# Moving one layer's transposes and a score turn from TensorE to VectorE and DRAM in a four-layer graph network kernel

## The chip, the cores and the metric

The kernel runs on one core of a Trainium2 chip. Its time is device time in microseconds (us), from start to end of one execution. The core has these engines: TensorE (PE in the profile; its weight loads are PEld), VectorE (DVE), ScalarE (ACT), GpSimd (POOL) and SyncE (SP), which here issues all DMA transfers. Each engine works through its own list of instructions in order, and a wait at the head of a list holds up what stands behind it.

## The reference

There are 64 graphs of 256 nodes with 256 features each, and an integer adjacency matrix per graph. Four layers follow each other; each normalises its input, cuts it at zero and adds its result to the state `x`:

```python
h = maximum(layernorm(x), 0); x = x + multihead_attention(h, adj)     # layer 0: 8 heads of 32
h = maximum(layernorm(x), 0); x = x + elu(softmax(mask(leaky(f1 + f2)), axis=1) @ (h @ W))   # layer 1
h = maximum(layernorm(x), 0); x = x + gated(h, adj)                   # layer 2
h = maximum(layernorm(x), 0); x = x + graph_attention(h, adj)         # layer 3: 4 heads of 64
# gated: three rounds of
m = h @ weight[i]; aggr = A.T @ m
r = sigmoid(i_r + h_r); z = sigmoid(i_z + h_z); n = tanh(i_n + r * h_n)
h = (1 - z) * n + z * h        # i_* = aggr @ w_ih.T + b_ih, h_* = h @ w_hh.T + b_hh
```

In layers 1 and 3 a score is the sum of a term of the row's node and a term of the column's node, so one of the two terms must stand along the free axis, on all partitions.

## The kernel before

Everything is float32. Two graphs form a pair, 32 pairs in all. A tile of one pair has 128 partitions and 4 token tiles of 256 features (1024 columns). A float32 matmul shows as two instructions in the trace, a transpose as one.

**The planner.** `Plan.add` records every step as a task with the engines that could do it, an estimated length, the buffers it reads and writes, and a stage name ("2n" is the norm of layer 2, "2z" its z gates). `Plan.order` (from L161) then writes out one order for the whole program: among the tasks that are ready and find free buffers it takes the one that can begin first by its estimates, and among equals the one with the lowest key, which is the pair times `PERIOD` plus a number from the table `KEYS` for stage and kind of engine. Work of several pairs is thus interleaved, and the buffer counts in `SLOTS` (with the spare ones that only the oldest pair may take) say how many pairs can be under way. `w4` are large buffers of 1024 columns, `w2` half ones of 512, `ps` the eight PSUM banks. `Plan.SWITCH` is the estimated price of changing the array mode of TensorE: L782 runs in row groups, L834 in column groups, L1234 in halves, the rest on the whole array.

**The norm.** `norm_relu` takes mean and variance on VectorE (L530, L532), the inverse root on GpSimd (L543, L544), and scales on ScalarE or VectorE (L557, L563). Then layers 0, 2 and 3 turn the tile to put features on partitions: eight 128x128 transposes on TensorE (L602) into two PSUM banks, and an eviction of each (L355 or L356, or with the relu L614 or L615). In layer 2 the relu comes before the turn, as the token form is needed too.

**Turning through DRAM.** The probabilities of layers 0 and 3, and in layer 2 the state between rounds, are turned without TensorE: VectorE transposes the 32x32 blocks of a tile (L672, L693, L1250), SP writes it to DRAM (L661, L1254), and four more transfers read it back with the blocks in their places (L664, L1257). Its readers then find the columns in runs of 32 elements ("mixed" in the code). The last pair turns its layer 2 state on TensorE (L1140).

**The score term.** `to_all` puts a column of scores on all partitions: a transpose on TensorE of 4, 8 or 16 columns (L859), an eviction (L355, L356), a store of the rows to DRAM (L864) and a load that repeats them on every partition (L872). Layer 1 calls it once a pair, layer 3 once, and twice in the last pair.

**Layer 2.** A round computes the bias part of n (stage 2h), sums messages over the graph (2m, L1036), then the gates r, n and z with L1059: eight instructions of 128x512 each for r and z and four each for the two parts of n, for each half `o` of the features. The n gate gets a sum (L1096), a tanh (L1100) and a subtraction h - n into a new tile `u` (L1105, VectorE or GpSimd); z gets a tanh (L1115) and two VectorE steps (L1120, L1125), which make `u` the new state.

Of the kernel before, what the change touches and what calls it, by code (L numbers as in the profile page):

```python
# [17 lines left out]
P = 128  # L18
EPS = 1e-5
MASKED = -1.0e30  # L20
ALPHA = 0.2
# [18 lines left out]
class Plan:  # L40
# [14 lines left out]
    SPARE, GRAIN = 5, 0.001  # L55
# [4 lines left out]
    PERIOD = 2008  # L60
# [3 lines left out]
        ("io", "SP"): -22628, ("w", "SP"): 6160, ("w", "on"): -16051, ("w", "PE"): 28184, ("0n", "on"): -19306,  # L64
        ("0n", "SP"): 5751, ("0n", "PE"): 4447, ("0", "on"): 13647, ("0", "PE"): -689, ("0s", "PE"): -30872,
        ("0s", "on"): 35014, ("0e", "on"): 15593, ("0e", "SP"): 64094, ("0c", "PE"): 582, ("0c", "on"): 67923,
        ("1n", "on"): 13111, ("1n", "SP"): -3349, ("1", "on"): 14867, ("1r", "PE"): 2956, ("1r", "on"): -22849,
        ("1r", "SP"): -28662, ("1e", "on"): 128, ("1c", "PE"): -14716, ("1c", "on"): -29044, ("2n", "on"): -12901,
        ("2n", "SP"): 36028, ("2n", "PE"): 3358, ("2", "on"): -7047, ("2h", "PE"): 8742, ("2h", "on"): 5862,
        ("2m", "on"): -11894, ("2m", "PE"): -1886, ("2r", "PE"): 8465, ("2r", "on"): -17986, ("2u", "PE"): 9750,  # L70
        ("2u", "on"): 12069, ("2z", "PE"): 10422, ("2z", "on"): -12469, ("2b", "on"): 642, ("2b", "SP"): 7700,
        ("3n", "on"): 25987, ("3n", "SP"): 33785, ("3n", "PE"): 6756, ("3", "on"): 2218, ("3", "PE"): -74722,
        ("3r", "on"): -55996, ("3r", "PE"): -624, ("3r", "SP"): 24892, ("3e", "on"): 40995, ("3e", "SP"): 20273,
        ("3c", "PE"): 10928, ("3c", "on"): 2398, ("3b", "on"): -8939, ("3b", "SP"): 23874, ("out", "SP"): -40141,
        ("2b", "PE"): 56777, ("3e", "PE"): -100101, ("3b", "PE"): 38324,
# [7 lines left out]
    def __init__(self, slots, spare):  # L83
        self.slots, self.spare = slots, spare
        self.pairs = []
        self.stage, self.rank = "", None
# [4 lines left out]
    def add(self, forms, reads=(), writes=(), latency=0.0, claims=(), mode="full"):  # L91
# [11 lines left out]
        t.stage, t.mode = self.stage, mode  # L103
# [31 lines left out]
    def order(self):  # L135
# [11 lines left out]
        for t in every:  # L147
            engine = t.forms[0][0]
            kind = engine if engine in ("PE", "SP") else "on"
            t.key = t.rank[0] * self.PERIOD + t.rank[1] * 1e-4 + self.KEYS.get((t.stage, kind), 0.0)  # L150
# [73 lines left out]
def tile_adj_preln_d4(  # L224
# [41 lines left out]
        "x": (5, [P, T * D], FP, 0),  # L266
        "w4": (24, [P, T * D], FP, 5),
        "part": (10, [P, N2], FR, 1),
        "f3": (2, [P, T, E3], FP, 0),
        "mask": (5, [P, T * N], BF, 0),  # L270
        "ps": (8, [P, 512], FP, 2),
        "w2": (4, [P, N2], FP, 1),
        "st": (4, [P, T, 6], FP, 0),
        "mv": (4, [P, T, 2], FP, 1),
        "rs": (4, [P, 2, T], FP, 2),
        "mx": (16, [P, H0], FP, 3),
        "zs": (12, [P, H0], FP, 3),
        "rz": (12, [P, H0], FP, 2),
        "f12": (2, [P, 2, T], FP, 0),
        "rows": (3, [T * H3, P], FP, 2),  # L280
        "dst": (4, [P, T, H3], FP, 3),
        "turn": (8, [P, T * N], FP, 3),
        "turn2": (4, [P, N2], FP, 2),
        "row1": (4, [N2], FP, 3),
        "row3": (4, [H3 * N2], FP, 0),
# [31 lines left out]
    for tag, (n, shape, dtype, _) in SLOTS.items():  # L317
        if tag not in tiles:
            tiles[tag] = [(dram if tag in ("row1", "row3", "turn", "turn2") else work).tile(shape, dtype, name=f"{tag}_{i}") for i in range(n)]
    plan = Plan({tag: v[0] for tag, v in SLOTS.items()}, {tag: v[3] for tag, v in SLOTS.items()})  # L320
# [4 lines left out]
    def w4():  # L325
        return buf("w4")
# [4 lines left out]
    def bank():  # L331
        return buf("ps")
# [183 lines left out]
    TURNED = ("2m",)  # L516
# [226 lines left out]
    def layer0(xt, p):  # L743
# [10 lines left out]
        qT, kT, v, cT = w4(), w4(), w4(), w4()  # L754
# [16 lines left out]
        for g in range(2):  # L771
# [55 lines left out]
            psc = bank()  # L827

            def context(g=g, psc=psc, pT=pT):
# [13 lines left out]
            add(  # L843
                evict(N2, lambda g=g: tok(cT(), N2)[:, :, g * N : (g + 1) * N], lambda psc=psc: tok(psc(), N)),
                reads=[psc], writes=[(cT, g)],
            )
            ps = bank()
            add((PE, 1.74, lambda ps=ps, g=g: graph_mm(ps, cT, wo_sb, g)), reads=[(cT, g), WO], writes=[ps])
# [6 lines left out]
    def to_all(row, src, columns, n, dsts):  # L855

        ps, rows = bank(), buf("rows")
        add(
            (PE, TURN + 0.12, lambda: nc.tensor.transpose(ps()[0:n, 0:P], columns(), ident)),  # L859
            reads=[src], writes=[ps], claims=[rows],  # L860
        )
        add(evict(P, lambda: rows()[0:n, :], lambda: ps()[0:n, 0:P]), reads=[ps], writes=[rows])
        add(
            (SP, 0.7, lambda: nc.sync.dma_start(row().rearrange("(c p) -> c p", p=P)[0:n], rows()[0:n, :])),  # L864
            reads=[rows], writes=[row], latency=1.8,
        )
        for i, dst in enumerate(dsts):

            def spread(i=i, dst=dst):
                n = dst().shape[1]  # L870
                part = row()[i * n : (i + 1) * n]
                nc.sync.dma_start(dst(), bass.AP(tensor=part.tensor, offset=part.offset, ap=[[0, P], [1, n]]))  # L872

            add((SP, 0.7, spread), reads=[row], writes=[dst], latency=4.2)

    def layer1(xt, p):
# [8 lines left out]
        for g in range(2):  # L885

            def dots(g=g):
                for t in (2 * g, 2 * g + 1):
                    for w in range(2):
                        nc.vector.tensor_tensor_reduce(  # L890
                            tok(e(), N)[:, t, :], tok(h())[:, t, :], wa_bc[:, w, :], 1.0, 0.0, ALU.mult, ALU.add, f12()[:, w, t : t + 1])

            add(
                (V, 4 * FUSED, dots, True), reads=[(h, g), W1], writes=[(e, 2 * g), (e, 2 * g + 1), (f12, g)],
            )
        f1 = buf("w2")
        plan.stage = "1r"
        to_all(buf("row1"), f12, lambda: f12()[:, 0], T, [f1])
        for t in range(T):
            g = t // 2  # L900
            add(
                (A, act(N, 1), lambda t=t, g=g: nc.scalar.activation(
                    tok(e(), N)[:, t, :], f1()[:, g * N : (g + 1) * N], AF.Prelu,
                    bias=f12()[:, 1, t : t + 1], alpha=ALPHA)),
                reads=[f1, f12], writes=[(e, t)],
            )
# [82 lines left out]
    def layer2(xt, p):  # L989
# [58 lines left out]
        for l in range(NL):  # L1048
            r, hn, u = w4(), w4(), w4()
# [15 lines left out]
            for o in range(2):  # L1065
                ps = gate(1.72, ((whhT, hT),), (4 + o) * P, o, [r, hn])
# [13 lines left out]
            for o in range(2):  # L1080
                ps = gate(3.44, both, o * P, o, [r])
                add(
                    (A, act(N2, 1), lambda o=o, ps=ps, r=r: nc.scalar.activation(  # L1083
                        at_o(r, o), ps(), AF.Tanh, bias=brz[:, o : o + 1], scale=0.5)),
                    reads=[ps, BN], writes=[(r, o)],
# [3 lines left out]
                        at_o(hn, o), at_o(r, o), 1.0, at_o(hn, o), ALU.add, ALU.mult), True),  # L1089
                    reads=[(r, o)], writes=[(hn, o)],  # L1090
                )
            plan.stage = "2u"
            for o in range(2):
                ps = gate(1.72, ((giT[:, l], aT),), (4 + o) * P, o, [u])
# [10 lines left out]
                    either(0.0, lambda eng, o=o, u=u, hT=hT, hn=hn: eng.tensor_sub(  # L1105
                        *((by_tile(wide(u, o)), wide(hT, o), by_tile(wide(hn, o))) if hT.mixed
                          else (wide(u, o), wide(hT, o), wide(hn, o))))),
                    reads=[hT if hT.mixed else (hT, o), (hn, o)], writes=[(u, o)],
                )

            plan.stage = "2z"
            for o in range(2):
                ps = gate(3.44, both, (2 + o) * P, o)
                add(
                    (A, act(N2, 1), lambda o=o, ps=ps, r=r: nc.scalar.activation(  # L1115
                        at_o(r, o), ps(), AF.Tanh, bias=brz[:, 2 + o : 3 + o], scale=0.5)),
                    reads=[ps], writes=[(r, o)],
                )
                add(
                    (V, dve(N2), lambda o=o, r=r, u=u: nc.vector.scalar_tensor_tensor(  # L1120
                        at_o(u, o), at_o(r, o), 1.0, at_o(u, o), ALU.add, ALU.mult), True),
                    reads=[(r, o)], writes=[(u, o)],
# [3 lines left out]
                        at_o(u, o), at_o(u, o), 0.5, at_o(hn, o), ALU.mult, ALU.add), True),  # L1126
# [5 lines left out]
            if by_dma("2m", p):  # L1132
                turn_chunks(u, h)
# [24 lines left out]
    def layer3(xt, p):  # L1158
# [29 lines left out]
        dst = buf("dst")  # L1188
        for ts, sds in ((slice(0, 2), sd[:1]), (slice(2, 4), sd[1:])) if hT.fine else ((slice(0, T), sd),):
            of = (dst, ts.start) if hT.fine else dst  # L1190
            add(
                (V, 0.09, lambda ts=ts: nc.vector.tensor_copy(dst()[:, ts], f()[:, ts, D + H3 : E3]), True),
                reads=[(f, t) for t in range(ts.start, ts.stop)], writes=[of],
            )
            n = (ts.stop - ts.start) * H3
            to_all(buf("row3"), of, lambda ts=ts: dst()[:, ts].rearrange("p t h -> p (t h)"), n, sds)
# [97 lines left out]
    for p in range(B // 2):  # L1294
        plan.pair()
        plan.stage, xt = "io", buf("x")
# [56 lines left out]
```

## Time and profile before

| | |
|---|---|
| median of 3 runs | 3545.06 us (3544.0 to 3546.97) |
| the profiled execution | 3550.16 us |
| its span, first to last instruction | 3548.4 us |
| granted TensorE clock, mean | 0.994 |
| DMA: read and written in DRAM | 394 MB and 281 MB, 190 GB/s over the span |
| TensorE's largest group, L1059 | 4608 instructions, 50% of the chain that ended last |

The durations in what follows come from that one profiled execution. A group's row gives line, engine, operation, result and operands by the program's names, shapes and count, then the group's busy time and the mean length of one in ns, then how long the engine stood idle before it and what ended that. Matmuls overlap each other, so a mean length can be more than busy time divided by count.

### The profile page before, as it was taken

The numbers are of one execution on the slowest core, as the hardware profiler recorded it, in microseconds if no ns is written. First come the engines' busy times: TensorE is split into PE (matmuls) and PEld (weight loads), VectorE is DVE, ScalarE is ACT, GpSimd is POOL, SyncE is SP. The second block draws the span as 40 slices with busy tenths as digits, with TensorE's granted clock in tenths as the row PEclk, the third lists the DMA queues.
The fourth block names the chain that finished last, engine by engine and source line by source line (L and its number), as shares of the span: only waits on it lengthen the run. The fifth ranks groups of instructions, "written<-read, shape, count | busy, mean of one in ns | idle before, by whom it ended". The sixth has DMA issues, their size and how long they took to land.

```text
span 3548.4 us, 54621 instructions
## 1 busy us (share of the span) xinstructions
PE 3500.6 (99%) x15345; PEld 1965.5 (55%) x15345; DVE 2879.5 (81%) x8769; ACT 2634.5 (74%) x7011; POOL 452.0 (13%) x505
## 2 busy tenths in 40 slices
PE   8999999999999999999999999999999999999996
PEld 5555555555555555555555555555555555555553
DVE  7887688887888878888887878888889887898655
ACT  7887576887678876787877778777788777778555
POOL 2001111111111110111101110011101011111010
PEclk9999999999999999999999999999999999999998
DMA  7755476665767656576565766657577565676534
GB/s 222 212 168 183 130 231 193 214 208 164 226 187 220 208 173 208 184 226 201 183 210 178 241 187 192 219 174 222 182 214 217 180 212 182 200 226 187 164 94 133
DMA packets 544142, 687.69 MB, mean 194 GB/s; under 512 B 86112, under 2 KB 463072, under 8 KB 543840
## 3 DMA queue, kind: packets, MB, share of 16 engines
q1 hardware_dynamic: 543840, 684.21, 63.2%
q8 instruction: 123, 2.02, 0.2%
q14 instruction: 179, 1.47, 0.2%
HBM read 394.28 MB, written 281.35 MB: 190 GB/s over the span
## 4 chain that ended last, share of the span: by engine, by line
PE 89%; DVE 4%; ACT 3%; DMA 2%; SPq 1%; issue 1%; POOL 0%; DVEq 0%; ACTq 0%; POOLq 0%
PE ps L1059 50%; PE ps L761 6%; PE ps L637 6%; PE ps L1036 5%; PE ps L782 4%; PE ps L1234 3%; PE ps L1179 3%; PE ps L834 3%; PE ps L966 3%; PE ps L952 3%; PE ps L602 2%; ACT w L737 1%; DVE w L730 1%; DVE w L672 1%; DMA x<-in_x_dram 1%
## 5 line engine op out<-in xcount | busy, mean ns | idle before, releaser
L1059 PE MATMUL ps<-w,whhT 128*128 128x512 f32 x2304 | 1078.6, 595 | 1.5 <-DVE w L1125 1.5
L1059 PE MATMUL ps<-w,giT 128*128 128x512 f32 x2304 | 1067.3, 592 | 0.0
L737 ACT ACTIVATE w<-w,mx 128x256 f32<-128x256 f32 x1536 | 758.9, 500 | 12.0 <-DVE mx L730 11.6
L1059 PEld LDWEIGHTS ps<-w,giT 128*128 128x128 f32 x2304 | 433.7, 190 | 530.6 <-issue 508.6
L1059 PEld LDWEIGHTS ps<-w,whhT 128*128 128x128 f32 x2304 | 424.0, 190 | 465.9 <-issue 426.3
L355 ACT COPY w<-ps 128x512 f32<-128x512 f32 x574 | 324.4, 581 | 275.1 <-PE ps L761 102.3
L672 DVE STREAM_TRANSPOSE w<-w 128x1024 f32<-128x1024 f32 x380 | 468.7, 1235 | 49.8 <-ACT w L814 30.4
L730 DVE CUSTOM_DVE_ANT_0 w<-ps,mask 128x256 f32<-128x256 f32 x1024 | 369.9, 416 | 54.2 <-PE ps L782 52.7
L814 ACT ACTIVATE w<-w,rz 128x256 f32<-128x256 f32 x672 | 292.8, 503 | 5.8 <-DVE rz L807 5.5
L737 ACT ACTIVATION_READ_ACCUMULATOR w<-w,mx 128x1 f32 x1536 | 295.9, 193 | 0.0
L543 POOL TENSOR_SCALAR rs<-mv 128x4 f32<-128x4 f32 x129 | 41.8, 324 | 1994.5 <-DVE mv L532 1919.4
L557 ACT ACTIVATE w<-x,rs 128x256 f32<-128x256 f32 x466 | 245.0, 591 | 50.3 <-DVE rs L549 50.1
L1115 ACT ACTIVATE w<-ps,brz 128x512 f32<-128x512 f32 x192 | 130.3, 679 | 148.1 <-PE ps L1059 148.1
L1211 ACT ACTIVATE w<-w,f 128x256 f32<-128x256 f32 x512 | 218.7, 498 | 15.8 <-DMA w<-row 15.8
L1036 PE MATMUL ps<-part,part 128*128 128x256 f32 x1536 | 226.0, 299 | 2.1 <-ACT part L1020 1.5
L730 DVE CUSTOM_DVE_ANT_0 w<-w,mask 128x256 f32<-128x256 f32 x512 | 201.9, 438 | 23.3 <-ACT w L1211 23.3
L1105 POOL TENSOR_TENSOR w<-w,w 128x512 f32<-128x512 f32 x84 | 112.8, 1344 | 809.2 <-ACT w L1100 634.6
L1036 PEld LDWEIGHTS ps<-part,part 128*128 128x128 f32 x1536 | 196.1, 191 | 35.6 <-issue 20.1
L1083 ACT ACTIVATE w<-ps,brz 128x512 f32<-128x512 f32 x192 | 130.1, 678 | 112.0 <-PE ps L1059 111.8
L1088 DVE SCALAR_TENSOR_TENSOR w<-w,w 128x512 f32<-128x512 f32 x192 | 136.4, 711 | 87.2 <-ACT w L1069 45.5
L1120 DVE SCALAR_TENSOR_TENSOR w<-w,w 128x512 f32<-128x512 f32 x192 | 141.5, 737 | 80.0 <-ACT w L1115 68.1
L1100 ACT ACTIVATE w<-w,bih_sb 128x512 f32<-128x512 f32 x192 | 135.3, 718 | 85.1 <-DVE w L1096 85.1
(116 smaller groups left out, 5122.1 us busy)
## 6 DMA issues: line engine op xcount, KB each, us to landing
turn<-w SPq DMA_DIRECT2D x473, 512.0 KB, 3.1
w<-turn SPq DMA_DIRECT2D x1892, 128.0 KB, 3.7
w<-in_adj_dram SPq DMA_DIRECT2D x128, 512.0 KB, 5.7
w<-row SPq DMA_DIRECT2D x64, 512.0 KB, 4.9
x<-in_x_dram SPq DMA_DIRECT2D x64, 256.0 KB, 4.3
out_dram<-x SPq DMA_DIRECT2D x64, 256.0 KB, 2.1
turn<-w SPq DMA_DIRECT2D x62, 256.0 KB, 2.0
w<-turn SPq DMA_DIRECT2D x248, 64.0 KB, 2.5
```

Of the source, the lines that this page charges most:

```text
L355: (A, act(n), lambda: nc.scalar.copy(dst(), src())),
L557: nc.scalar.activation(tok(xn())[:, t, :], tok(xt())[:, t, :], func, bias=rs()[:, 1, t : t + 1], scale=rs()[:, 0, t : t + 1])
L637: mm(ps()[:, c * D : (c + 1) * D], chunk(src, k, 2 * g + c), rhs[:, k, :], start=k == 0, stop=k == 1)
L672: add((V, dve(T * N), lambda: nc.vector.transpose(blocks(), blocks())), writes=[e])
L730: nc.vector.tensor_tensor_reduce(row, src, mask, scale, 3.0e38, ALU.add, ALU.min, mn)
L737: nc.scalar.activation(row(e, r), row(e, r), AF.Exp, bias=mn()[:, r : r + 1], scale=-1.0, accum_out=zs()[:, z0(r) : z0(r) + 1])
L761: mm(ps(), w[:, k, o * P : (o + 1) * P], wide(hT, k), start=k == 0, stop=k == 1)
L782: mm(banks[hh]()[:, cc * N : (cc + 1) * N], tok(qT(), N2)[r, cc, t * P : (t + 1) * P], tok(kT(), N2)[r, cc, g * N : (g + 1) * N].rearrange ...
L814: op(row, row, rz()[:, r : r + 1])
L1036: mm(ps()[:, o * N : (o + 1) * N], chunk_of(part(), h.mixed, c, o), tok(ams[g](), N)[:, c, :], start=i == 0 and c == 0, stop=i == 1 and c ...
L1059: mm(ps(), w[:, k, c0 : c0 + P], wide(src, k), start=n == 0, stop=n == 2 * len(terms) - 1)
L1211: nc.scalar.activation(dst, src, AF.Prelu, bias=f()[:, t, D + h : D + h + 1], alpha=ALPHA)
```

## The change

For all pairs but the last, the norm of layer 2 turns its tile with the function `turn_rows`, which was there but not used: a block transpose on VectorE and a trip through DRAM; the two evictions fall away. The gates of round 0 then read the turned tile in runs of 32, and `u` is a tile of its own in that round only; in the others the new state is written over the old one. `to_all` no longer uses TensorE: VectorE transposes the blocks of a 128x32 tile and the store to DRAM picks 32-element runs out of it. The results of the r and z gates go to half buffers, the z gates are listed ahead of the second part of the n gate, and the context of layer 0 goes to a half buffer per graph. Buffer counts, spares, `PERIOD` and all keys are new, and the first pair and the last two have keys of their own.

```diff
-    SPARE, GRAIN = 5, 0.001
+    SPARE, GRAIN = 2, 0.001
...
-    PERIOD = 2008
+    PERIOD = 2538
...
-        ("2u", "on"): 12069, ("2z", "PE"): 10422, ("2z", "on"): -12469, ("2b", "on"): 642, ("2b", "SP"): 7700,
...
+        ("2r<", "on"): -6234, ("2z<", "PE"): 8380, ("2z<", "on"): -1814, ("2u<", "PE"): 8044, ("2u<", "on"): -10808,
...
-            t.key = t.rank[0] * self.PERIOD + t.rank[1] * 1e-4 + self.KEYS.get((t.stage, kind), 0.0)
+            t.key = t.rank[0] * self.PERIOD + t.rank[1] * 1e-4 + self.KEYS.get((t.stage, kind), self.KEYS.get((t.stage.strip("<>"), kind), 0.0))
...
-        "x": (5, [P, T * D], FP, 0),
-        "w4": (24, [P, T * D], FP, 5),
+        "x": (6, [P, T * D], FP, 0),
+        "w4": (22, [P, T * D], FP, 2),
...
-        "mask": (5, [P, T * N], BF, 0),
+        "mask": (6, [P, T * N], BF, 1),
...
-        "w2": (4, [P, N2], FP, 1),
+        "w2": (5, [P, N2], FP, 0),
...
-        "f12": (2, [P, 2, T], FP, 0),
-        "rows": (3, [T * H3, P], FP, 2),
-        "dst": (4, [P, T, H3], FP, 3),
+        "f12": (2, [P, 32], FP, 0),
+        "rows": (3, [P, 32], FP, 2),
+        "dst": (4, [P, 32], FP, 3),
...
-    TURNED = ("2m",)
+    TURNED = ("2", "2m")
...
-        qT, kT, v, cT = w4(), w4(), w4(), w4()
+        qT, kT, v = w4(), w4(), w4()
...
-            psc = bank()
+            psc, cT = bank(), buf("w2")
...
-        ps, rows = bank(), buf("rows")
+        rows = buf("rows")
+        add((V, 0.11, lambda: nc.vector.transpose(rows(), src())), reads=[src], writes=[rows])
         add(
-            (PE, TURN + 0.12, lambda: nc.tensor.transpose(ps()[0:n, 0:P], columns(), ident)),
-            reads=[src], writes=[ps], claims=[rows],
-        )
-        add(evict(P, lambda: rows()[0:n, :], lambda: ps()[0:n, 0:P]), reads=[ps], writes=[rows])
-        add(
-            (SP, 0.7, lambda: nc.sync.dma_start(row().rearrange("(c p) -> c p", p=P)[0:n], rows()[0:n, :])),
-            reads=[rows], writes=[row], latency=1.8,
+            (SP, 0.7, lambda: nc.sync.dma_start(row().rearrange("(j a i) -> a j i", a=4, i=32), rows())),
+            reads=[rows], writes=[row], latency=2.2,
         )
...
-            r, hn, u = w4(), w4(), w4()
+            hn = w4()
...
+                r = buf("w2")
...
+            plan.stage = "2z"
+            zt = [buf("w2") for o in range(2)]
+            for o in range(2):
+                ps = gate(3.44, both, (2 + o) * P, o, [zt[o]])
...
             plan.stage = "2u"
+            u = w4() if hT.mixed else hT
...
-                    reads=[hT if hT.mixed else (hT, o), (hn, o)], writes=[(u, o)],
-                )
...
+                    reads=[(hn, o), *([hT] if hT.mixed else [])], writes=[(u, o)],
+                )
+                add(
+                    (V, dve(N2), lambda o=o, z=zt[o], u=u: nc.vector.scalar_tensor_tensor(
+                        wide(u, o), z(), 1.0, wide(u, o), ALU.add, ALU.mult), True),
+                    reads=[zt[o]], writes=[(u, o)],
+                )
...
+        plan.place = "<" if p == 0 else ">" if p >= B // 2 - 2 else ""
```

The function that the norm of layer 2 now calls:

```python
    def turn_rows(xn):

        e, eT = w4(), w4()
        add(
            (V, dve(T * D), lambda: nc.vector.transpose(
                e().rearrange("p (b x i) -> p x b i", b=4, i=32), xn().rearrange("p (x b j) -> p x b j", b=4, j=32))),
            reads=[xn], writes=[e],
        )
        through_dram(e, eT)
        eT.mixed = True
        return eT
```

## The prediction

> **What bounds the kernel now.** I read the busy shares first, then the busy times by stretch of the span, then TensorE's groups, its timeline, and last the waits.
>
> ```profile
> PE 3500.6 (99%) x15345; PEld 1965.5 (55%) x15345; DVE 2879.5 (81%) x8769; ACT 2634.5 (74%) x7011; POOL 452.0 (13%) x505
> ```
>
> TensorE is busy for 99% of the span, VectorE for 81%. Whether TensorE is bound everywhere is told by the stretches (columns: stretch, its length, then busy time and instructions of each engine, granted clock, DMA share, GB/s):
>
> ```profile
> 0.00:50.00 50.00, 38.06 (x187) 25.84 (x188) 32.79 (x136) 33.85 (x92) 19.65 (x26) 0.93 0.73 232
> 300.00:3300.00 3000.00, 2997.38 (x13074) 1673.85 (x13072) 2483.09 (x7525) 2249.28 (x5985) 391.64 (x431) 1.00 0.65 199
> 3450.00:3548.40 98.40, 71.15 (x292) 39.58 (x290) 57.88 (x176) 57.67 (x156) 9.38 (x12) 0.85 0.48 145
> ```
>
> From 300 to 3300 us TensorE stands still for 2.6 us in 3000, at clock 1.00; VectorE has 17% free, ScalarE 25%, the DMA engines 35%. There time is bought only by giving TensorE less to do. The last 98.4 us hold 27.2 us of idle TensorE, the first 50 hold 11.9: at the ends a chain of single steps decides. The order repeats every 430.6 us for four pairs (the long runs of L1059 start at 1522.50, 1953.13, 2383.77 in the chain), 107.65 us a pair; 32 such are 3444.8, so 103.6 us of the span are ends, weights among them.
>
> **TensorE work that goes.** Two kinds of transpose:
>
> ```profile
> L602 PE MATMUL ps<-ident,w 128*128 128x128 f32 x768 | 104.0, 278 | 12.8 <-ACT w L557 12.7
> ...
> L859 PE MATMUL ps<-ident,f 128*4 128x128 f32 x32 | 8.7, 272 | 0.0
> L859 PE MATMUL ps<-ident,dst 128*16 128x128 f32 x31 | 8.5, 273 | 0.0
> ```
>
> L602 is the norm's transpose in layers 0, 2 and 3: 32 pairs x 3 x 8 = 768. Layer 2's go through VectorE for all pairs but the last: 31 x 8 = 248. A mean of 278 ns is not what one costs, as matmuls overlap; what counts is from start to next start (columns: start, length, engine, line, operation):
>
> ```profile
> 1450.54 1.04 PE L602 MATMUL ps<-ident,w 128*128 128x128 f32 x8
> 1451.41 1.88 PE L1059 MATMUL ps<-w,giT 128*128 128x512 f32 x4
> ```
>
> ```profile
> 3468.58 0.27 PE L859 MATMUL ps<-ident,dst 128*16 128x128 f32 x1
> 3468.69 1.88 PE L1059 MATMUL ps<-w,whhT 128*128 128x512 f32 x4
> ```
>
> Eight take 0.87 us, 0.109 each; one of L859 takes 0.11. The Trainium skill speaks otherwise: "TensorE: Matmul & The Clock Gate", Part 4 (PE-mode transpose), gives about 275 ns for one in a kernel's context. The row has that as a duration, but not as spacing. By 275 ns the 248 + 65 transposes would be 86 us; by the timeline 31 x 0.87 = 27.0 us and 65 x 0.11 = 7.2 us, together **34.2 us**. I take the timeline, since in the saturated stretch the next start is what moves.
>
> **What VectorE, ScalarE and DMA get.** The turned tile costs a block transpose, a write of 512 KB to DRAM and four reads, as the tiles at L672 do now:
>
> ```profile
> L672 DVE STREAM_TRANSPOSE w<-w 128x1024 f32<-128x1024 f32 x380 | 468.7, 1235 | 49.8 <-ACT w L814 30.4
> ```
>
> 31 x 1.235 = 38.3 us on VectorE. The score columns get a 128x32 block transpose; no row has one, so it lies between the 128x16 copy (L1192, 174 ns) and the 128x512 block transpose (L1250, 701 ns); I take 0.2 us as the nearer: 13 us. Gone are 11 copies of rows there (3 us). VectorE comes to about 2879 + 38 + 13 - 3 = 2927 us, 84% of 3505. ScalarE loses 54 copies of rows (13 us) and most of the 62 evictions of 0.58 us: a turned tile of layer 2 had its relu before, and needs none after. Both stay under TensorE, so this costs nothing while their order leaves TensorE fed; were VectorE the bound, it would be +48 us.
>
> A rule speaks against the change: "VectorE: DVE Perf Modes", Rules for kernel authors, sends a 128x128 transpose to TensorE where PSUM will do as its destination. Counting engine time it is right here too: 38.3 us on VectorE for 27.0 on TensorE, a loss of 11. But a free 17% pays for a full 100%, so the sum takes -27.
>
> DMA: 31 x 1 MB = 32.5 MB on 688, near 5%; at 63% busy that makes 66%. SP issues 31 x 5 more, at 0.34 us (write) and 0.43 us (read) each 64 us in all; the block transposes' waits on SP are of the kind it has (L661 behind L672: 582.5 us in 231 waits), and queued behind them are other pairs' loads, whose tiles lie ready early. The rows' stores become 128 pieces of 128 B instead of 4 or 16 of 512 B; landing took 3.0 us and I take 3 to 4, off the path except at the end, where it is +1 against the 1.5 us that the transpose and copy took there (3510.10 to 3511.63).
>
> **A slower operand?** In round 0 of 31 pairs the gates read the turned tile in runs of 32 elements: 31 x 24 = 744 instructions of 0.429 us (L1059: four in 1.72), 319 us. Nearest is L1234, which reads turned probabilities in such runs, two matmuls of 256 columns at a time: 32 took 3.61 us. The dense L637 of 256 columns takes 1.73 for eight, 0.216 each, so 32 dense ones two at a time would take 3.46. The 0.15 between them I put down to the change of array mode, since the dense-reading L782 shows such a loss too. So I take zero. If all of that 4% were the runs', it is +14 us; a gain is excluded, since L1059's dense reads are as fast per column as any row has them.
>
> **State in place, smaller buffers, order.** Rounds 1 and 2 (and 0 of the last pair) now write h - n over h, so that subtraction waits until all z gates have read h; before, it could run ahead. Behind it wait two VectorE operations of its own (L1120 and L1125, 0.74 and 0.70), and on an in-order engine whatever is queued next. The z gates' tanh (0.68) runs beside it, so one round gets 0.1 to 0.7 us longer. Hidden where other pairs feed TensorE; in the last pair I count +2. Gates of r and z move from 24 large buffers to 5 half ones, shared with the context tile: more takers, but short ones; I take zero, and the order rival holds the rest. Changes of array mode: an excursion (L782, L834, L1234) costs about 0.3 us beyond its matmuls (16 of L782, four at a time: 1.07 where 16 x 0.216/4 is 0.86, and 0.09 to enter), and the timeline from 1496 to 1873 has about 6.5 of at most 8 a pair. The new keys may merge or split some: one per pair is 32 x 0.3 = 10 us either way; zero taken.
>
> **The ends.** What TensorE waited for there:
>
> ```profile
> PE ps L602 <- ACT w L557: 12.7, 2, 8.8
> PE ps L682 <- ACT w L737: 12.1, 6, 8.3
> PE ps L1140 <- DVE w L1125: 5.9, 2, 3.8
> ```
>
> The 8.8 is the first load and stays. On the chain of the last 60 us I can name what another order would remove: the z tanh waiting behind exponentials (3492.5 to 3494.4, 1.9), the row load behind a turned tile's store on SP (3514.6 to 3515.8, 1.2), GpSimd for an add that VectorE does in half (0.6), the row path (1.5, less 1 for the pieces); in the first 130 us, waits of 2.1, 1.2 and 0.7. That is 8.2, say 8. Bounds: a lengthening of 4, the in-place chain's 2 and as much again from the order, and at best 20, about half of the 39 us idle in both stretches. I take -8 + 2 = **-6**.
>
> **Sum.** On the profiled execution (3550.16 us, span 3548.4): -27.0 - 7.2 - 6 = -40.2, to 3510. It lay 5.1 us above the median of the runs; from 3545.06 the same sum gives **3505 us**.
>
> **Rivals.** (1) As summed, ends between +4 and -18: 3493 to 3515, 0.58. (2) The strided reads do cost: 3505 + 14 = 3519, 0.16; for it, that no full-array matmul reads so yet; against it, L1234. (3) The order gains more: two excursions a pair merged, or the ends halved, 3505 - 19 = 3486, 0.19; for it, 103.6 us at the ends; against it, that two score groups together need all eight PSUM banks. (4) Slower: the turned tile comes late. The path is 1.24 + 3.1 + 3.7 us and queueing, against some 2 us, so about 8 us later; with nothing else to do TensorE would lose 31 x 8 = 248 us, and 3545 - 40 + 248 = 3753. It decides from 40.2/31 = 1.3 us of lost time a pair. Against it stand the turned tiles there are:
>
> ```profile
>   PEld ps L1234: 3.5, 6
>   PEld ps L834: 3.4, 5
> ```
>
> In 535 such tiles TensorE's loads waited 6.9 us, 0.013 each, so 31 more are 0.4 us. For it: SP is in order, and buffers of the large kind are fewer. 0.07: slower 0.04, the same 0.02, still faster 0.01.
>
> **Numbers.** A run can tell about 0.2% (7 us) from no change. Cases 1 to 3 are all faster: 0.93 + 0.01. The range 3482 to 3522 leaves out the high end of (2) and the low end of (3), 0.05 each, and (4): 0.17.
>
> **What would show it.** L602 falls to 520, L859 is gone, TensorE's matmul count falls by 313; the repeat falls from 430.6 to 4 x (107.65 - 0.87 - 0.22) = 426.2 per four pairs, less or more by excursions; four strided L1059 still start 1.72 us apart; VectorE near 84%; idle TensorE still under 5 us between 300 and 3250. Waits of TensorE on the turned tile, a repeat above 430, or a last stretch longer than now would prove me wrong.

## The result and the profile after

The changed kernel takes 3518.77 us in the median (3518.36 to 3519.41, 4 runs), the kernel before 3545.71 us beside it (4 runs): a ratio of 0.9924, 95% interval 0.9907 to 0.9942. That is 27 us less; 40 were forecast. The profiled execution took 3519.16 us with a span of 3517.4. The busy times of the engines after:

```profile
PE 3457.1 (98%) x15032; PEld 1944.5 (55%) x15032; DVE 2873.1 (82%) x8732; ACT 2674.8 (76%) x7097; POOL 347.9 (10%) x435
```

TensorE has 313 instructions less, as many as were to go, but its idle time has not shrunk: 3517.4 - 3457.1 is 60.3 us, against 47.8 before. The stretches of the span after, with the columns as before:

```profile
0.00:50.00 50.00, 41.39 (x190) 27.73 (x191) 34.67 (x134) 31.83 (x81) 21.16 (x28) 1.00 0.75 242
50.00:300.00 250.00, 229.98 (x1145) 134.73 (x1144) 203.99 (x658) 185.29 (x524) 12.91 (x16) 0.97 0.61 186
300.00:3300.00 3000.00, 2998.21 (x13031) 1681.12 (x13030) 2503.53 (x7586) 2338.83 (x6200) 297.31 (x372) 1.00 0.67 211
3450.00:3517.40 67.40, 39.04 (x157) 21.36 (x155) 36.91 (x124) 41.65 (x119) 5.91 (x7) 0.76 0.41 131
```

The second row has to be seen beside the same stretch of the kernel before:

```profile
50.00:300.00 250.00, 245.79 (x1292) 147.13 (x1291) 215.36 (x701) 210.48 (x594) 22.39 (x27) 0.99 0.68 200
```

From 300 to 3300 us TensorE is as full as it was. Between 50 and 300 us it now idles 20.0 us for 4.2, and its granted clock is 0.97 for 0.99. What became of the transposes, in TensorE's and VectorE's groups after (L627 is L602 before; L731 and L889 are the new block transposes):

```profile
L627 PE MATMUL ps<-ident,w 128*128 128x128 f32 x520 | 70.9, 279 | 14.1 <-ACT w L582 14.0
...
L731 DVE STREAM_TRANSPOSE w<-w 128x1024 f32<-128x1024 f32 x31 | 38.3, 1236 | 0.8 <-ACT w L582 0.8
...
L889 DVE STREAM_TRANSPOSE rows<-dst 128x32 f32<-128x32 f32 x33 | 6.8, 206 | 0.3
L889 DVE STREAM_TRANSPOSE rows<-f 128x32 f32<-128x32 f32 x32 | 6.5, 202 | 0.0
```

768 transposes have become 520, the score transposes (L859 before) are gone, and the small block transpose takes 0.2 us. The repeat, read from the chain of work that ended last (start, length, what):

```profile
1009.73 24.04 PE ps L1087 x56
1048.74 20.60 PE ps L1087 x48
1115.75 24.04 PE ps L1087 x56
```

The order now repeats with every pair, each 106.02 us, for 107.65 before: 1.63 us less where 1.09 was to go. And 56 instructions of L1087 still take 24.04 us, 0.429 each. The strided reads of round 0 are no slower: from 500 to 3000 us no L1087 that follows another starts more than 0.434 us after it.

**An account of TensorE's time.** To see where the time went I count, in stretches of 50 us, each matmul at its spacing in a full stretch (512 columns 0.429 us, 256 columns 0.216, 264 columns 0.223, the graph sums of L1036 or L1064 0.126, row and column groups 0.054, halves 0.108, transposes 0.109, and so on), and call that useful; the rest of the stretch is lost, be it idle, a changed mode or a lower clock. (Those graph sums run in the type fp32r, so not everything in the kernel is plain float32.) An excursion is a run of matmuls in row groups, column groups or halves; the first gate is the start of L1059 or L1087 for the first pair.

| us | useful | lost to 300 us | lost 300 to 3300 | lost after 3300 | mode excursions, 500 to 3000 us | first layer 2 gate |
|---|---|---|---|---|---|---|
| before | 3398.2 | 35.6 | 69.9 | 44.6 | 151 | 141.0 |
| after | 3364.0 | 54.4 | 54.9 | 44.1 | 117 | 172.9 |
| difference | -34.2 | +18.8 | -15.0 | -0.5 | | |

The sum is -30.9, and the spans differ by 31.0. The useful work falls by just the 34.2 us forecast because the count prices the transposes at the same 0.109 us: it shows that the work is gone, and e5 below tests the price. The lost time fell by 15.0 in the middle and rose by 18.8 at the start.

### The profile page after: what moved, and what is told of

Its sections match the earlier page's. It is cut to its first block, busy times and chain, and to the rows that moved or that the text cites. A ratio compares the mean times of both kernels' runs of the same rounds, so it can differ in the third digit from the quotient of the medians.

```text
span 3517.4 us, 54023 instructions
## 1 busy us (share of the span) xinstructions
PE 3457.1 (98%) x15032; PEld 1944.5 (55%) x15032; DVE 2873.1 (82%) x8732; ACT 2674.8 (76%) x7097; POOL 347.9 (10%) x435
## 4 chain that ended last, share of the span: by engine, by line
PE 90%; DVE 2%; ACT 1%; DMA 1%; issue 0%; SPq 0%; POOL 0%; DVEq 0%; ACTq 0%
PE ps L1087 54%; PE ps L1064 5%; PE ps L786 5%; PE ps L807 3%; PE ps L1209 3%; PE ps L1263 3%; PE ps L980 3%; PE ps L859 3%; PE ps L994 3%; PE ps L662 3%; PE ps L874 3%; PE ps L627 1%; DMA w<-turn 1%; DVE w L755 0%; ACT w L762 0%; DVE w L697 0%
## 5 line engine op out<-in xcount | busy, mean ns | idle before, releaser
L1087 PE MATMUL ps<-w,whhT 128*128 128x512 f32 x2304 | 1067.7, 593 | 1.5 <-DMA w<-turn 1.5
L1087 PE MATMUL ps<-w,giT 128*128 128x512 f32 x2304 | 1058.3, 592 | 0.7 <-ACT w L380 0.7
L1087 PEld LDWEIGHTS ps<-w,giT 128*128 128x128 f32 x2304 | 436.8, 190 | 544.6 <-issue 527.9
L1087 PEld LDWEIGHTS ps<-w,whhT 128*128 128x128 f32 x2304 | 426.2, 190 | 467.5 <-issue 430.9
L380 ACT COPY w<-ps 128x512 f32<-128x512 f32 (+1 forms) x519 | 295.1, 580 | 290.7 <-PE ps L786 119.3
L839 ACT ACTIVATE w<-w,rz 128x256 f32<-128x256 f32 x782 | 341.9, 508 | 4.5 <-DVE rz L832 4.4
L1135 DVE TENSOR_TENSOR w<-ps,w 128x512 f32<-128x512 f32 x192 | 129.4, 674 | 209.1 <-PE ps L1087 208.5
L568 POOL TENSOR_SCALAR rs<-mv 128x4 f32<-128x4 f32 x129 | 32.5, 252 | 2703.1 <-DVE mv L557 2680.1
L582 ACT ACTIVATE w<-x,rs 128x256 f32<-128x256 f32 x492 | 257.4, 605 | 16.3 <-DVE rs L574 16.1
L1064 PE MATMUL ps<-part,part 128*128 128x256 f32 x1536 | 236.5, 303 | 5.3 <-DVE part L1022 4.3
L1064 PEld LDWEIGHTS ps<-part,part 128*128 128x128 f32 x1536 | 199.5, 190 | 41.2 <-issue 28.2
L755 DVE CUSTOM_DVE_ANT_0 w<-w,mask 128x256 f32<-128x256 f32 x512 | 195.4, 427 | 18.8 <-ACT w L1240 16.6
L555 DVE BATCH_NORM_STATS2 st<-x 128x6 f32<-128x256 f32 x512 | 188.8, 410 | 2.8 <-DMA x<-in_x_dram 2.3
L1117 DVE SCALAR_TENSOR_TENSOR w<-w,w 128x512 f32<-128x512 f32 x192 | 130.3, 679 | 60.5 <-ACT w L1112 58.0
```

The costliest lines, as they stand in the source:

```text
L380: (A, act(n), lambda: nc.scalar.copy(dst(), src())),
L555: nc.vector.bn_stats(st()[:, t, :], tok(xt())[:, t, :])
L582: nc.scalar.activation(tok(xn())[:, t, :], tok(xt())[:, t, :], func, bias=rs()[:, 1, t : t + 1], scale=rs()[:, 0, t : t + 1])
L755: nc.vector.tensor_tensor_reduce(row, src, mask, scale, 3.0e38, ALU.add, ALU.min, mn)
L839: op(row, row, rz()[:, r : r + 1])
L1064: mm(ps()[:, o * N : (o + 1) * N], chunk_of(part(), h.mixed, c, o), tok(ams[g](), N)[:, c, :], start=i == 0 and c == 0, stop=i == 1 and c ...
```

## The experiments

The theories: (A) useful work and lost time add up, and the new loss at the start comes from the new order; (B) the turned tile's trip through DRAM makes it, or takes back what TensorE saves; (C) the first pair's own keys make it; (D) the keys are fitted to one program, and a disturbed order loses TensorE time, whatever is moved. (D) was formed after the first four runs. The figures of lost time in the expectations come from an earlier count that took matmuls on a stretch's border twice; it had 117 where the table's sum is 150 for the kernel before, and the differences are much the same. Every run below has the kernel before beside it on its chip, at 3546 to 3547 us.

| run | median us | ratio, 95% interval | lost to 300 | 300 to 3300 | after 3300 | first gate |
|---|---|---|---|---|---|---|
| e1 parts only | 3656.21 | 1.0306 (1.0288 to 1.0323) | 51.4 | 173.1 | 69.2 | 152.9 |
| e2 unturned | 3607.67 | 1.0172 (1.0157 to 1.0188) | 45.0 | 121.1 | 48.9 | 156.2 |
| e3 first pair as middle | 3607.29 | 1.0170 (1.0154 to 1.0185) | 54.0 | 138.3 | 50.7 | 172.6 |
| e4 last pairs as middle | 3525.45 | 0.9941 (0.9926 to 0.9956) | 53.3 | 53.9 | 53.3 | 171.9 |
| e5 dummy turns | 3542.80 | 0.9989 (0.9982 to 0.9995) | 50.2 | 53.2 | 43.0 | 172.0 |
| e6 other period | 3624.22 | 1.0214 (1.0199 to 1.0229) | 33.9 | 134.3 | 54.9 | 139.6 |
| e7 mode switch | 3540.40 | 0.9986 (0.9977 to 0.9994) | 53.3 | 67.8 | 44.4 | 171.1 |
| e8 control of e7 | 3533.03 | 0.9960 (0.9946 to 0.9975) | 55.4 | 60.0 | 42.9 | 175.0 |
| e9 parts, keys anew | 3544.80 | 0.9993 (0.9983 to 1.0003) | 50.2 | 80.1 | 48.1 | 146.0 |
| e10 first on TensorE | 3527.69 | 0.9946 (0.9931 to 0.9961) | 46.4 | 65.9 | 45.1 | 156.1 |
| e11 VectorE twice | 3542.32 | 0.9990 (0.9980 to 0.9999) | 58.4 | 75.7 | 44.6 | 175.2 |

**e1: the two moves alone.** The kernel before with `to_all` on VectorE as changed, and

```diff
-    TURNED = ("2m",)
+    TURNED = ("2", "2m")
```

> The kernel before with only the two transposes moved (layer 2's tile, score columns), its own keys, buffers and gate order. Theory A (useful TensorE work and lost time add up; the loss at the start comes from the new order, not from the moved work): 34 us less useful work, lost time stays near 117 us, first layer 2 gate near 141 to 150 us, 3511 us. Theory B (the turned tile's trip through DRAM delays layer 2 at the start): lost time before 300 us rises from 33 to about 52, first gate near 165 to 175, 3530 us.

Measured 3656 us: slower than before by 110, and both theories are wrong. The useful work is 3363.4, as low as after the change, so the saving is there; but the middle loses 103 us more than in the kernel before; 60 of it is idle TensorE (2937.2 us busy for 2997.4), and its granted clock there was 0.99 for 1.00. Of what TensorE waited for in its first 300 us, the second row is new:

```profile
PE ps L605 <- ACT w L560: 8.6, 1, 8.6
PE ps L1058 <- DMA w<-turn: 7.4, 1, 7.4
```

The first gate of layer 2 waits once, 7.4 us, for the turned tile. From 300 to 3300 us the longest waits are of other kinds. None of the gates waits on the tile, but the context of layer 3 (L1232) waits on turned probabilities, and no matmul of it did before:

```profile
PE ps L1058 <- DVE w L1124: 12.3, 6, 4.4
PE ps L605 <- ACT w L560: 9.4, 7, 7.4
PE ps L1035 <- DVE part L993: 9.0, 7, 3.2
PE ps L1232 <- DMA w<-turn: 6.0, 3, 4.4
```

**e2: the changed kernel with the tile back on TensorE** (`TURNED = ("2m",)`).

> The changed kernel with layer 2's tile turned on TensorE again (248 transposes come back), all else as changed. Theory A: 27 us more useful work, the start as in the changed kernel (first gate near 173, about 52 us lost before 300), 3546 us. Theory B: the start recovers (first gate near 145, 33 us lost), so 27 - 19 = +8, 3527 us.

Measured 3608 us, 62 more than (A) has. The start recovers by 9.4 us, half of the 18.8, so there (B) is half right. The middle loses 66 us more, though layer 2's tile no longer goes to DRAM: this loss cannot be its trip's.

**e3: no own keys for the first pair** (the weights keep theirs).

```diff
-        plan.place = "<" if p == 0 else ">" if p >= B // 2 - 2 else ""
+        plan.place = ">" if p >= B // 2 - 2 else ""
```

> The changed kernel without the first pair's own keys (it takes those of the middle pairs; weights keep theirs). Theory C (those keys hold layer 2 of the first pair back): first gate before 160 us, lost before 300 us near 35, about 3500 us. Theory A with the cause in depth and middle keys: the start stays as bad or gets worse, 3519 to 3535 us. Steady period 106.0 us in both.

Measured 3607 us with the same work in every instruction, and the period was not kept. The start is unchanged (54.0, first gate 172.6), so (C) falls. The keys of one pair cost 88 us, nearly all of it hundreds of us later. TensorE's busy time in the middle of e3:

```profile
1000.00:2000.00 1000.00, 982.01 (x4226) 548.72 (x4225) 824.44 (x2488) 760.44 (x2024) 138.27 (x151) 1.00 0.68 208
```

and of the changed kernel in the same stretch:

```profile
1000.00:2000.00 1000.00, 1000.00 (x4373) 563.49 (x4372) 834.68 (x2562) 794.57 (x2120) 93.27 (x119) 1.00 0.68 215
```

In e3 147 instructions fewer get done in the 1000 us. By the code of `Plan.order` each choice depends on what came free before, so another start can lead to another sequence for good; that this is the path is argued, and the trace shows the later loss alone.

**e4: no own keys for the last two pairs** (`plan.place` only for the first).

> The changed kernel without the own keys of the last two pairs. If they earn their keep: lost time after 3300 us rises from 41 to over 50, about 3530 us. If they do nothing: within 5 us of 3519. The start and the period of 106.0 us stay.

Measured 3525 us, 6.7 more than with these keys. The two intervals overlap, but the count puts the difference at the end: it loses 53.3 us without them and 44.1 with them, as the kernel before does.

**e5: eight transposes put back at a fixed order.** In the order of the changed kernel, ahead of a gate of round 0:

```diff
+                    if extra:
+                        for j in range(8):
+                            nc.tensor.transpose(ps()[:, (j % 4) * P : (j % 4 + 1) * P], h0()[:, j * P : (j + 1) * P], ident)
```

> The changed kernel in its own order, with eight extra 128x128 transposes on TensorE in 31 pairs, into a bank that the matmuls after them overwrite; the planner does not know of them. Theory A (in a full stretch the spacing of 0.109 us is the price): 31 x 0.87 = +27 us, 3546 us, period 106.0 + 0.87. If a duration of 275 ns each were the price: +68 us, 3587. If TensorE were not the bound: under +5 us.

Measured 3542.8 us, +24 of the 27 expected. The chain gives the period:

```profile
1013.48 24.04 PE ps L1090 x56
1120.36 24.04 PE ps L1090 x56
```

It is 106.88 us, 0.86 more, for eight transposes at 0.109. So in the full stretch the spacing is the price, and not the length of 275 ns.

**e6: the kernel before with another `PERIOD`** (2100 for 2008, no work changed).

> The kernel before with the planner's PERIOD at 2100 for 2008: no work is changed, only the order. Theory D (the keys are fitted to one program, and any disturbance of the order loses TensorE time in the middle, whatever the work): useful work stays at 3432 us, lost time rises from 117 by 40 or more, 3590 us or above. Theory B' (the loss seen when the parts are put in alone comes from the turned tile's wait on DRAM): within 10 us of 3546.

Measured 3624 us: 78 us for one number of the planner, useful work 3398.7, 64 us more lost in the middle. What (D) expected comes, without any moved work. Not every change of keys does it, though: e4 left the middle as it was.

**e7 and e8: the price of an excursion.** One extra small matmul ahead of four gates a pair, in e7 on a column group, in e8 on the whole array:

```diff
+                        mm(ps()[0:32, 0:32], h0()[:, 0:32], h0()[:, 0:32], start=True, stop=True)
```

> The changed kernel in its own order, with four extra excursions to column groups a pair (one 32x32 matmul ahead of four gates, overwritten after), unknown to the planner: 128 in all. At 0.3 us each: +38 us, 3557 us. If excursions cost nothing beyond their matmuls: +5 us or less, as its control.

> The control: the same 128 extra small matmuls on the whole array, no change of mode. +0.06 us each or less: 3519 to 3527 us.

Measured 3540.4 and 3533.0 us, periods 106.77 and 106.46 for 106.02. Both expectations miss: a small matmul on the whole array already costs 0.44/4 = 0.11 us, one on a column group 0.19, so the mode adds 0.08 over its control. A lone small matmul is not a pack of 32, though. What such a pack costs is read from the timeline of the kernel before:

```profile
1473.44 1.04 PE L602 MATMUL ps<-ident,w 128*128 128x128 f32 x8
1474.41 1.93 PE L834 MATMUL ps<-w,w 128*32 128x256 f32 x32
1476.27 3.83 PE L1179 MATMUL ps<-w3a,w 128*128 128x264 f32 x16
1479.93 1.89 PE L637 MATMUL ps<-wo_sb,w 128*128 128x256 f32 x8
```

and of the changed kernel, where both graphs' contexts run as one:

```profile
1300.26 3.60 PE L1087 MATMUL ps<-w,giT 128*128 128x512 f32 x8
1303.79 3.66 PE L859 MATMUL ps<-w,w 128*32 128x256 f32 x64
1307.38 1.99 PE L662 MATMUL ps<-wv_sb,w 128*128 128x256 f32 x8
```

Before, the 32 begin 0.10 us after the eight transposes' 0.87 us are over, they take 1.86 us for 32 x 0.054 = 1.73, and the 16 of L1179 behind them take 3.66 for 16 x 0.223 = 3.57: together 0.3 us beyond the work. The 64 have the same 0.10 to enter and take 3.59 for 3.46. In the median from 500 to 3000 us, entry and leaving included, an excursion costs 0.33 us with 32 matmuls (35 cases before) and with 64 (23 cases after). So the price is one per excursion, a merge saves 0.33 us, and the prediction's 0.3 was right in size. (It was read from L782's row groups, which cost 0.40 in the same count, as what follows them runs 0.10 late; the prediction left that out.) Excursions fell from 6.5 a pair (151 in 2500 us) to 5.0 (117): 1.5 x 0.33 = 0.5 us, which with 0.87 + 0.22 for the transposes makes 1.59 of the 1.63 us of the period.

**e9: the moves alone, with keys searched anew.** The kernel of e1, with the buffers and gate order of the kernel before; no pair has keys of its own.

> The kernel of e1 (the kernel before with only the two transposes moved, its buffers and gate order) with keys searched anew for it, and no own keys for any pair. Theory D (the loss of e1 was the unfitted order): lost time falls from 258 to 110 to 140 us, useful work stays 3399, so 3509 to 3540 us. Theory B (the trip through DRAM takes back what TensorE saves): still above 3546.

Measured 3544.8 us: no different from the kernel before (interval 0.9983 to 1.0003). The new keys took away 111 us of e1's time, so the unfitted order was most of what e1 lost. But useful work is 34.2 us lower than before and lost time 28.3 higher: 14.6 at the start, 10.2 in the middle, 3.5 at the end. The first gate waits for the tile again:

```profile
PE ps L1104 <- DMA w<-turn: 8.1, 1, 8.1
```

**e10: the first pair's tile on TensorE.** The changed kernel with

```diff
-        return l in TURNED and p < B // 2 - 1
+        return l in TURNED and p < B // 2 - 1 and (l != "2" or p >= 1)
```

and keys searched anew.

> The changed kernel with the first pair's layer 2 tile turned on TensorE (0.9 us more useful work) and keys searched anew from its own. Theory B for the start only (the first turned tile comes late when no other pair can feed TensorE): first gate before 165 us, lost before 300 us falls from 52 to 40 to 47, 3508 to 3514 us. Otherwise within 3 us of 3519.

Measured 3527.7 us. At the start it fits (B): 8.0 us less lost, first gate at 156. But the middle lost 11.0 more, and the whole took 8.9 us more than the change in the median (5.1 in the profiled spans; the intervals overlap), where up to 11 less was expected: a miss. Its keys are others throughout, so the 8.0 us are not the tile's alone.

**e11: the block transpose done twice at a fixed order** (31 x 1.23 us more on VectorE).

> The changed kernel in its own order, with the block transpose of layer 2's tile done twice: 31 x 1.23 = 38 us more on VectorE. If free VectorE time pays for it, as the prediction has it: period 106.0, under +6 us in all, most of it at the start. If VectorE's order were on the path: +20 to +38 us.

Measured 3542.3 us, +23.6: the prediction's view fails here. The period is 106.84, 0.82 more, two thirds of what was added. The timeline of TensorE in e11 shows where:

```profile
1184.19 1.88 PE L1088 MATMUL ps<-w,whhT 128*128 128x512 f32 x4
1185.90 0.42 PE L627 MATMUL ps<-ident,w 128*128 128x128 f32 x2
1186.49 0.33 PE L627 MATMUL ps<-ident,w 128*128 128x128 f32 x1 [0.17 <-ACT w L582]
1186.98 0.77 PE L627 MATMUL ps<-ident,w 128*128 128x128 f32 x5 [0.16 <-ACT w L582]
1187.58 1.88 PE L1088 MATMUL ps<-w,whhT 128*128 128x512 f32 x4
```

and the same place in the changed kernel:

```profile
1279.50 1.88 PE L1087 MATMUL ps<-w,whhT 128*128 128x512 f32 x4
1281.21 1.04 PE L627 MATMUL ps<-ident,w 128*128 128x128 f32 x8
1282.09 1.88 PE L1087 MATMUL ps<-w,whhT 128*128 128x512 f32 x4
```

The eight transposes of a norm take 1.68 us for 0.88, as they wait for ScalarE's scaling (L582), which waits for the statistics on VectorE. Everything ahead of them in the period stands at the same distance to 0.01 us. In the changed kernel VectorE runs from 1261.8 to 1281.7 us without a gap ahead of this place, and the new block transpose (1272.66) is in that run. So added VectorE time there moves the norm's statistics, the scaling and then TensorE.

## Why the prediction was right or wrong, point by point

**The total is near the forecast in part by luck.** Between the profiled executions it is -30.9 us for -40.2. The 9.3 us between them are 24.3 missed at the ends less 15.0 in the middle that were taken at zero; that the two misses offset each other was not foreseen.

**The bound and the saved work were right.** TensorE is full from 300 to 3300 us, 313 transposes are gone, and e5 puts 0.86 us a pair back for the 0.87. The Trainium skill's 275 ns ("TensorE: Matmul & The Clock Gate", Part 4) is what one takes from start to end here too (279 in L627's row), and not what a full TensorE saves.

**The strided reads cost nothing**, as taken (0.434 us at most between neighbours). The measured 3519 lies on the number of that rival, but not by its cause.

**"The ends: -6" failed.** They became +18.3, all at the start. I listed waits that another order could remove and did not ask how the new path of the first pair's tile would sit there, though my own rival (4) said that it comes about 8 us later where TensorE has nothing else. In e1 and e9 the first gate waits 7.4 and 8.1 us for it. In the changed kernel about half of the 18.8 us goes when that tile is turned on TensorE (9.4 by e2, 8.0 by e10), but TensorE's waits in the first 300 us show less of it at the gate itself (second row) than at the context of layer 0, which waits for turned probabilities:

```profile
PE ps L859 <- DMA w<-turn: 6.0, 4, 3.8
PE ps L1087 <- DMA w<-turn: 1.5, 1, 1.5
```

In e2 the first row is 2.1 us, and in the kernel before no matmul waits so. All these tiles go through SP's one list; that layer 2's trip holds up the others there is likely, and was not shown. The other half is in the new order's start or in the score turn, which e2 keeps (45.0 for 35.6), and not in the first pair's keys, by e3. The split is not firm: e1 and e9 lose 15.8 and 14.6 us more at the start with the old buffers and gate order. Which of score turn, buffers, spares and middle keys makes the rest was not tried and stays open. At the end the own keys of the last two pairs are worth 6.7 us in the median (9.2 by the count), and that only held the loss where it was.

**"Changes of array mode: zero taken" was mis-sized.** The price was near, the count was not: with 1.5 excursions a pair fewer at 0.33 us, the 28 pairs of the middle give an estimated 14 us, and 15.0 less were lost there. The sum works out: -34.2 - 15.0 + 18.3 = -30.9.

**"A free 17% pays for a full 100%" failed as a rule.** VectorE's 38.3 and 13 us came as forecast, and TensorE stayed full. But the planner had also moved 110 divisions to ScalarE (782 in L839 for 672 in L814 before), and VectorE ended at 82%, not 84. At the fixed order two thirds of the VectorE time added in e11 shows in the period. So the other rule ("VectorE: DVE Perf Modes", Rules for kernel authors: TensorE for a 128x128 transpose where PSUM will do) was not as far off as I said: moved with the old buffers and gate order and the best keys that I found, the transposes gain nothing (e9), though it was not shown that VectorE is what takes the gain back there.

**"Buffers and gate order: zero taken" can't be kept.** Between e9 and the changed kernel lie 26 us, with the same moves. They come from the new buffers, the gate order, the state in place, the context in half buffers, own keys and another search for keys, together; the parts were not told apart, since one alone can disturb the order by more than it is worth (e2, e3, e6). Nor was the kernel before run with new buffers and keys and its transposes left on TensorE, so how much of the 27 us a better fit alone would have given stays open.

**Rival (4)**, the late tile, decides at the start only. In the full stretch no gate waited for it, neither in the changed kernel nor in e1; in e1 other turned tiles came late there (6.0 us).

## What to carry to other kernels

In a saturated stretch, cost a removed instruction by the distance between starts, and check the sum with a count of useful work, since useful and lost time move apart. Where a planner lays out the order, treat the order as a part of the kernel: put in a change alone, and it is timed with a wrong order; refit before judging. Here the new keys of e9 were worth 111 us and the whole change 27. An engine at 82% has no slack where its list runs without a gap ahead of what the full engine waits for (e11); look at that stretch, not at the share.

## What the runs showed of the hardware

A small matmul on the whole array between large ones cost 0.11 us (e8), and one on a column group 0.19 (e7), where 0.06 was expected of the first. An excursion of 32 or 64 column-group matmuls cost 0.33 us beyond its work: 0.09 to enter, 0.14 inside and 0.10 behind it. TensorE's granted clock fell to 0.90 between 150 and 200 us of the changed kernel, where it idled 10 of 50 us, and it was 1.00 in the full stretch.
